# A perceiver kernel on one core: router scatters split into pairs, and the scale and bias of the contexts' layer norm given to GpSimd

## The chip, the core and the metric

The kernel runs on one core of a Trainium2 chip. The metric is the device time of one execution in microseconds (us). An execution moves through five engines that have their own instruction queues and wait for each other by semaphores: TensorE (PE in the profile; its weight loads are PEld), VectorE (DVE), ScalarE (ACT), GpSimd (POOL) and SyncE (SP), which here only issues DMA transfers. Each engine takes its instructions in the order in which the program lists them: an instruction that has to wait holds everything behind it on that engine.

## The reference

The inputs are latents x of 64 batches of 32 rows of 256 numbers, and for each batch a context of 257 rows of 256. In float32 the reference computes six residual steps in a row:

```python
x = x + cross_attention_1(context, norm(x))   # 16 heads of 64, with layer norms, q and k normed
x = x + self_attention_1(norm(x))             # 16 heads of 16
x = x + mixture_of_experts(norm(x))           # router: 8 of 64 experts a row, and a shared expert
x = x + cross_attention_2(norm(x), context)   # 16 heads of 64, softmax
x = x + self_attention_2(norm(x))             # latent heads, causal
x = x + ffn(norm(x))
```

Two pieces of it matter here. In the first cross-attention every context row is normed and then scaled and shifted by two vectors g and b of 256 numbers:

```python
def layernorm(x, g, b, eps=1e-05):
    m = jnp.mean(x, axis=-1, keepdims=True)
    v = jnp.mean((x - m) ** 2, axis=-1, keepdims=True)
    return (x - m) / jnp.sqrt(v + eps) * g + b
```

In the mixture of experts a router chooses 8 experts for each of the 2048 rows, and the row is copied to a slot of each chosen expert:

```python
w, idx = jax.lax.top_k(probs, TOP_K)
buf = jnp.zeros((E, CAPACITY + 1, H), x.dtype).at[e_flat, slot].set(x[tok])
```

## The kernel before

The 2048 latent rows are 16 tiles (t) of 128 rows, so four batches to a tile. The program has three stages. `before` does the first cross-attention batch by batch, and in its gaps the first self-attention and the router, tile by tile. `experts` runs the 64 experts and the shared one. `after` does the rest. The change lies in `before`.

The loop of `before` runs over the 64 batches (s; the profile's tiles name a batch's context `cx`). It is a software pipeline whose order is written out by hand. In step s it issues: the keys of batch s+2 (`keys`: 16 products of L180 into `psA`, copied by ACT at L1256 and DVE at L1258 into `kT`, squared by ACT at L1261 into `sq`); the transposes of batch s's softmaxed scores (`weigh`, L220, copied at L221); the norms of the keys of s+2 (`norms`: PE L1273, then DVE L1281, then ACT L1282); the values of batch s (`values`: PE L234 and L244); the spread of those norms (`spread`: PE L1294, then ACT L1295); the transposes of context s+3 (`turn`: PE L1228, ACT L1231, and two small copies by POOL at L1232 and L1233); the scores of s+2 (PE L1313, DVE L1323 and L1324, and the softmax with DVE L195, ACT L197, DVE L200 and L203, then DVE L210 and ACT L208); and last `prepare(s + 4)`, the layer norm of the context of s+4. So a context that is prepared in step s is transposed in step s+1.

`prepare` takes a context as two blocks of 128 rows by 256. DVE takes the statistics (L143, L145, L132), ACT makes 1/sqrt(variance) out of them (L133, L134), and then DVE makes four passes of 128x256: for each block L1215 subtracts the mean and multiplies by g, and L1216 multiplies by 1/sqrt and adds b.

The rest of the work hangs in between as Python generators. `slot()` goes once through the lists `tails` and `fronts` and runs each generator to its next `yield`. A front makes the queries of a coming tile (`queries`: DVE L154, POOL L1148 and L1149, DVE L1168 and L1169, POOL L1177, and the mask with POOL L1199 to L1201). A tail is what is left of a tile: the output product and its bias (POOL L185, DVE L186), self-attention (POOL L560 among it), and last `route`. Once the router's probabilities are there, `route` counts the slots (POOL L648), makes 8 row numbers (DVE L651 to L664, the last of them `fi`) and issues 8 scatters of 128 rows from POOL's queue (L667).

The order on PE is the program's own order. On the other engines a list scheduler of the language layer reorders the instructions at build time by its own estimates and by priorities (`with self.urgent()` raises one). It also chooses between DVE and ACT for copies that are written as `nc.any`. What the order on DVE, ACT and POOL becomes is thus not seen in the source.

Of the kernel before, what the change touches and what calls it, by code (L numbers as in the profile page):

```python
# [14 lines left out]
ALU = mybir.AluOpType  # L15
AX = mybir.AxisListType

P = 128
D = 256
# [14 lines left out]
TOPK = 8  # L34
# [67 lines left out]
class Kernel:  # L102
# [506 lines left out]
    def route(self, t, gw):  # L609
        nc = self.nc  # L610
        z, zT = yield from self.normed(t)
        nc.sync.dma_start(self.zs[t // GT][:, :, t % GT, :], zT)
        ps = self.bank("psA")
        self.product(
            ps[:, : E + 1],
            [zT[:, k, :] for k in range(2)],
            [gw[:, k, :] for k in range(2)],
        )

        sgt = self.sgate[:, t : t + 1]  # L620
        nc.scalar.activation(sgt, ps[:, E : E + 1], AF.Exp, scale=-1.0)
        nc.vector.tensor_scalar(sgt, sgt, 1.0, None, ALU.add)
        nc.vector.reciprocal(sgt, sgt)
        mx = self.small.tile([P, 1], F32, name="mx1")
        sm = self.small.tile([P, 1], F32, name="sm1")
        nc.vector.tensor_reduce(mx, ps[:, :E], AX.X, ALU.max, negate=True)
        pr = self.wk.tile([P, E], F32, name="pr")
        nc.scalar.activation(pr, ps[:, :E], AF.Exp, bias=mx, accum_out=sm)
        nc.vector.reciprocal(sm, sm)
        nc.vector.tensor_scalar(pr, pr, sm, None, ALU.mult)  # L630
        top = self.small.tile([P, TOPK], F32, name="top")
        nc.vector.max(top, pr)
        sel = self.wk.tile([P, E], F32, name="sel")
        nc.vector.match_replace(sel, top, pr, -1.0)
        nc.vector.tensor_scalar(sel, sel, 0.0, None, ALU.is_lt)
        tot = self.small.tile([P, 1], F32, name="tot")
        nc.vector.tensor_reduce(tot, top, AX.X, ALU.add)
        nc.vector.reciprocal(tot, tot)
        nc.vector.tensor_scalar(pr, pr, tot, None, ALU.mult)

        yield
        yield

        ps = self.bank("psA")
        self.product(ps[:, :E], [self.tri, self.ones], [sel, self.count])
        kept = self.wk.tile([P, E], F32, name="kept")
        nc.vector.scalar_tensor_tensor(kept, ps[:, :E], float(CAP), sel, ALU.is_lt, ALU.mult)
        nc.gpsimd.tensor_tensor(self.count, self.count, sel, ALU.add)  # L648
        val = self.wk.tile([P, E], F32, name="val")
        nc.vector.tensor_tensor(val, ps[:, :E], self.slot, ALU.add)  # L650
        nc.vector.tensor_tensor(val, val, kept, ALU.mult)  # L651
        v8 = self.small.tile([P, TOPK], F32, name="v8")
        nc.vector.max(v8, val)
        junk = self.wk.tile([P, E], F32, name="junk")
        for k in range(TOPK):
            nc.vector.scalar_tensor_tensor(
                junk, val, v8[:, k : k + 1], pr, ALU.is_equal, ALU.mult, accum_out=self.w8[:, t, k : k + 1]
            )
        nc.vector.tensor_copy(self.idx[:, t, :], v8)
        far = self.small.tile([P, TOPK], F32, name="far")  # L660
        nc.vector.tensor_scalar(far, v8, 0.0, FAR, ALU.is_equal, ALU.mult)
        nc.vector.tensor_tensor(far, far, v8, ALU.add)
        fi = self.small.tile([P, TOPK], I32, name="fi")
        nc.vector.tensor_copy(fi, far)  # L664

        for k in range(TOPK):
            d = nc.gpsimd.indirect_dma_start(  # L667
                out=self.buf[:, :],
                out_offset=bass.IndirectOffsetOnAxis(ap=fi[:, k : k + 1], axis=0),
                in_=z[:, 0, :],  # L670
                in_offset=None,
                bounds_check=E * CAP,
                oob_is_err=False,
            )
            self.tc.declare_no_dep(d.ins, group="scatter", reason="rows differ")
            self.tc.add_to_no_dep_group("scatter", d.ins)

    def experts(self, ctx, slot, tails):
        tc, nc, a = self.tc, self.nc, self.a
# [449 lines left out]
class CrossFirst:  # L1129
# [79 lines left out]
    def prepare(self, s):  # L1209

        k, nc, cx = self.k, self.k.nc, self.cx[s]
        mv, rs = k.stats(cx, 2)
        for j in range(2):
            x = cx[:, j, :]
            nc.vector.scalar_tensor_tensor(x, x, mv[:, j, 0:1], self.gx, ALU.subtract, ALU.mult)  # L1215
            nc.vector.scalar_tensor_tensor(x, x, rs[:, j : j + 1], self.bx, ALU.mult, ALU.add)  # L1216

    def turn(self, s):

# [308 lines left out]
```

## Time and profile before

| what | value |
|---|---|
| median of three runs | 2818.46 us (2815.7 to 2818.79) |
| the profiled execution, own time | 2816.43 us |
| its span, first to last instruction | 2814.2 us |
| mean granted TensorE clock | 0.984 |
| busy share of the span: PE, PEld, DVE, ACT, POOL | 94%, 65%, 62%, 44%, 19% |

The profile is one execution, so durations of single instructions come from it. The stage that the change touches lies between 0 and about 1465 us; the experts follow it. "Idle before, releaser" in a view says which instruction ended an engine's wait. PE is the engine to watch: a microsecond on another engine counts only where PE comes to wait for it. One tile of four batches takes 94 us in the middle of the stage, so one batch takes about 23.6 us.

### The profile page before, as it was taken

What the parts mean: (1) busy time and instruction counts of PE and PEld (TensorE: products, weight loads), DVE (VectorE), ACT (ScalarE), POOL (GpSimd) and SP (SyncE); (2) the same over time, 40 slices, a digit from 0 to 9 for tenths busy, and PEclk for the clock granted to TensorE, in tenths of its full rate; (3) what the DMA queues carried; (4) which work ended last, traced back from release to release, by engine and by line L of the source; (5) the groups of instructions that cost most, each with busy time, mean ns of one, the idle gap of its engine ahead of it and who ended that gap; (6) DMA issues with size and microseconds to landing.
All of it is one profiled execution on the core that took longest, in us unless ns stands there. A gap on an engine that the chain in (4) does not pass through costs nothing. (4 is left out here: it accounts for less than half of the span.)

```text
span 2814.2 us, 59449 instructions
## 1 busy us (share of the span) xinstructions
PE 2657.5 (94%) x23642; PEld 1824.2 (65%) x23642; DVE 1737.1 (62%) x4557; ACT 1235.0 (44%) x3474; POOL 541.5 (19%) x644
## 2 busy tenths in 40 slices
PE   6999999999999999999997889899999999999995
PEld 4566656665666566656664578677777777777763
DVE  6565656665666567656754533556666666666664
ACT  4555555555555555555553333333333333333331
POOL 3110122112211221122112200421222222121001
PEclk9999999999999999999998999999999999999997
DMA  7000001001110000000002388221212222221110
GB/s 262 27 16 14 18 31 33 31 18 31 32 30 18 27 26 22 18 19 19 17 5 86 130 270 269 83 72 48 61 48 58 52 55 59 51 57 47 33 33 7
DMA packets 136088, 157.05 MB, mean 56 GB/s; under 512 B 24024, under 2 KB 118979, under 8 KB 135812
## 3 DMA queue, kind: packets, MB, share of 16 engines
q1 hardware_dynamic: 114308, 119.65, 13.8%
q0 software_dynamic: 12288, 25.21, 3.5%
q10 hardware_dynamic: 9216, 8.39, 0.9%
q8 instruction: 187, 3.06, 0.5%
q14 instruction: 89, 0.73, 0.1%
HBM read 121.63 MB, written 37.75 MB: 57 GB/s over the span
## 5 line engine op out<-in xcount | busy, mean ns | idle before, releaser
L180 PE MATMUL psA<-xT,wk 128*128 128x289 f32 x2048 | 528.0, 413 | 16.6 <-issue 12.3
L180 PEld LDWEIGHTS psA<-xT,wk 128*128 128x128 f32 x2048 | 386.7, 192 | 151.6 <-issue 46.2
L828 POOL DMA_INDIRECT y<-oute,idx x128 | 131.0, 1024 | 646.2 <-DVE x L839 466.5
L234 PE MATMUL psY<-at,cx 128*128 128x512 f32 x512 | 237.6, 607 | 0.0
L180 PE MATMUL psY<-xT,qk 128*128 128x257 f32 x1024 | 233.7, 381 | 0.0
L180 PE MATMUL psA<-at,cx 128*128 128x512 f32 x512 | 233.5, 599 | 0.0
L180 PEld LDWEIGHTS psY<-xT,qk 128*128 128x128 f32 x1024 | 190.0, 190 | 25.2
L1414 ACT ACTIVATE sim<-psY,mx 128x257 f32<-128x257 f32 x256 | 120.6, 476 | 149.0 <-DVE mx L1413 148.0
L234 PEld LDWEIGHTS psY<-at,cx 128*128 128x128 f32 x512 | 92.6, 191 | 122.4 <-issue 99.0
L197 ACT ACTIVATE sim<-sim,mx 128x289 f32<-128x289 f32 x256 | 135.5, 532 | 63.9 <-DVE mx L195 63.7
L180 PEld LDWEIGHTS psA<-at,cx 128*128 128x128 f32 x512 | 93.4, 190 | 96.5 <-issue 83.2
L1261 ACT ACTIVATE sq<-kT 128x1156 f32<-128x1156 f32 x128 | 148.5, 1160 | 11.6 <-DVE kT L1258 10.5
L246 ACT COPY yT<-psY 128x512 f32<-128x512 f32 x128 | 68.7, 589 | 191.0 <-PE psY L244 191.0
L1323 DVE TENSOR_TENSOR sim<-psB,sim 128x289 f32<-128x289 f32 x256 | 100.8, 451 | 81.1 <-remote 27.9
L1256 ACT COPY kT<-psA 128x289 f32<-128x289 f32 x256 | 99.2, 388 | 116.8 <-PE psA L180 114.7
L667 POOL DMA_INDIRECT buf<-z,fi x128 | 126.3, 986 | 96.2 <-DVE fi L664 53.9
L1258 DVE COPY kT<-psA 128x289 f32<-128x289 f32 x256 | 114.5, 450 | 45.3 <-PE psA L180 45.0
L1413 DVE TENSOR_REDUCE mx<-psY 128x1 f32<-128x257 f32 x256 | 100.9, 417 | 52.9 <-PE psY L180 52.7
L180 PE MATMUL psY<-yT,wv 128*64 128x128 f32 x2048 | 126.3, 275 | 7.3 <-DVE yT L1444 7.3
L180 PEld LDWEIGHTS psY<-yT,wv 128*64 128x64 f32 x2048 | 114.9, 137 | 16.3 <-DVE yT L1444 11.2
L186 DVE TENSOR_TENSOR x<-x,psY 128x256 f32<-128x256 f32 (+1 forms) x80 | 29.2, 364 | 154.0 <-PE psY L180 152.4
L180 PE MATMUL psY<-wo,oT 128*128 128x128 f32 (+1 forms) x768 | 124.2, 315 | 0.0
(262 smaller groups left out, 5021.2 us busy)
## 6 DMA issues: line engine op xcount, KB each, us to landing
cx<-in_ctx SPq DMA_DIRECT2D x128, 256.0 KB
we<-in_m_ew SPq DMA_DIRECT2D x64, 384.0 KB
xT<-in_ctxT SPq DMA_DIRECT2D x64, 257.0 KB
buf<-zero SPq DMA_DIRECT2D x32, 256.0 KB
be<-buf SPq DMA_DIRECT2D x64, 128.0 KB
oute<-oe ACTq DMA_DIRECT2D x64, 128.0 KB
mu<-in_mask SPq DMA_DIRECT2D x16, 128.5 KB
x<-in_x SPq DMA_DIRECT2D x16, 128.0 KB
```

The lines of the kernel that those rows point to most:

```text
L180: self.nc.tensor.matmul(ps, lhsT=lhs[i], rhs=rhs[i], start=(i == 0), stop=(i == n - 1))
L197: nc.scalar.activation(sim[:, g, :], sim[:, g, :], AF.Exp, bias=mx[:, g : g + 1], accum_out=sm[:, g : g + 1])
L234: nc.tensor.matmul(ps[kc], lhsT=values[i][:, kc * P : (kc + 1) * P], rhs=at[i], start=(i == 0), stop=(i == n - 1 and tail is None),)
L246: nc.any.tensor_copy(yT[:, kc, :, b * S : (b + 1) * S], ps[kc].rearrange("p (h i) -> p h i", h=H))
L667: d = nc.gpsimd.indirect_dma_start(out=self.buf[:, :], out_offset=bass.IndirectOffsetOnAxis(ap=fi[:, k : k + 1], axis=0), in_=z[:, 0, :], ...
L828: nc.gpsimd.indirect_dma_start(out=y, out_offset=None, in_=self.oute[:, :], in_offset=bass.IndirectOffsetOnAxis(ap=self.idx[:, t, k : k + ...
L1256: nc.scalar.copy(kT[:, p, :], ps[:, :JK])
L1258: nc.vector.tensor_copy(kT[:, p, :], ps[:, :JK])
L1261: nc.scalar.activation(sq[p // 4], kT[:, p - 3 : p + 1, :], AF.Square)
L1323: nc.vector.tensor_tensor(sim[:, g, :], ps[i][:, :JK], sim[:, g, :], ALU.mult)
L1413: nc.vector.tensor_reduce(mx[:, g : g + 1], ps[:, :J], AX.X, ALU.max, negate=True)
L1414: nc.scalar.activation(sim[:, g, :], ps[:, :J], AF.Exp, bias=mx[:, g : g + 1], accum_out=sm[:, g : g + 1])
```

## The change

Two edits. The first puts a `yield` behind the second, fourth and sixth scatter of a tile, for all tiles but the last two. The second replaces the four DVE passes of `prepare`. DVE norms each block in one pass through the common helper (`layernorm`, whose pass is L154 in the profile before), and POOL then multiplies both blocks by g in one instruction of 128x512, and adds b in another.

```diff
@@ route
             self.tc.add_to_no_dep_group("scatter", d.ins)
+            if k % 2 and k < TOPK - 1 and t < self.nt - 2:
+                yield
@@ CrossFirst.prepare
         k, nc, cx = self.k, self.k.nc, self.cx[s]
-        mv, rs = k.stats(cx, 2)
-        for j in range(2):
-            x = cx[:, j, :]
-            nc.vector.scalar_tensor_tensor(x, x, mv[:, j, 0:1], self.gx, ALU.subtract, ALU.mult)
-            nc.vector.scalar_tensor_tensor(x, x, rs[:, j : j + 1], self.bx, ALU.mult, ALU.add)
+        k.layernorm(cx, cx)
+        nc.gpsimd.tensor_tensor(cx, cx, self.gx.unsqueeze(1).to_broadcast([P, 2, D]), ALU.mult)
+        nc.gpsimd.tensor_tensor(cx, cx, self.bx.unsqueeze(1).to_broadcast([P, 2, D]), ALU.add)
```

The two POOL instructions stand at L1215 and L1216 of the changed source, the lines that the four DVE passes had before; between the two edits all line numbers are two higher.

## The prediction

> **What bounds the kernel now.** I read the page first, then the stage that the change touches in one window, then PE's waits in it.
>
> ```profile
> PE 2657.5 (94%) x23642; PEld 1824.2 (65%) x23642; DVE 1737.1 (62%) x4557; ACT 1235.0 (44%) x3474; POOL 541.5 (19%) x644
> 100.00:1465.00 1365.00, 1330.86 (x11345) 849.67 (x11347) 885.92 (x2464) 734.62 (x2031) 271.29 (x354) 0.99 0.08 22
> PE psA L180 <- issue: 11.5, 33, 0.7
> PE psB L1313 <- ACT qTf L1193: 6.7, 15, 1.7
> PE psB L1273 <- ACT sq L1261: 5.7, 8, 1.0
> PE psT L163 <- issue: 3.8, 6, 1.0
> PE psB L1313 <- issue: 3.5, 11, 0.4
> PE psA L180 <- ACT xT L1231: 2.2, 4, 0.7
> PE psB L594 <- ACT yT L246: 0.2, 1, 0.2
> ```
>
> The window row gives the busy time of PE, PEld, DVE, ACT and POOL in 1365 us: PE 97.5%, DVE 65%, POOL 20%. The rows below it are all of PE's waits in that window (us in total, times, longest): 33.6 us. None names POOL, none names DVE. So the stage is PE's, and nothing that makes DVE lighter can win more than part of 33.6 us, while whatever makes PE's suppliers late costs at once. The next question is how late a supplier may be.
>
> ```profile
> 641.09 1.18 PE L1273 MATMUL psB<-sq,c 128*32 128x289 f32 x16
> 643.06 0.45 DVE L1281 TENSOR_SCALAR nk<-psB 128x289 f32<-128x289 f32 x1
> 643.55 0.45 ACT L1282 ACTIVATE nk<-nk 128x289 f32<-128x289 f32 x1 [1.76 <-DVE nk L1281]
> 646.89 0.77 PE L1294 MATMUL psR<-nk,c 32*128 32x289 f32 x8
> ```
>
> These four rows of the timeline (start, duration) are the chain of the key norms in the batch of a tile in which the router runs. ACT is done at 644.00, PE needs it at 646.89: 2.89 us in hand. In the batch before it (L1282 at 620.15, L1294 at 622.90) it is 2.30 us. All else that DVE hands over is asked for a batch (23.6 us) later.
>
> **First edit: the scatters.** In the built program's POOL order the eight scatters of every tile still stand in one row, before and after: the scheduler puts them together whatever the yields say. So it does nothing to PE, whose order is the same instruction for instruction. What remains: a tail lives three slots longer and holds `z` and `fi` longer; z's buffer is next wanted some four slots later, and the last two tiles, which the experts wait for, are exempt. Price 0. Were a `z` held too long, DVE's next L154 would wait; I give that 2 us at most, and no gain, since POOL sat idle 77 us before these scatters in the window.
>
> **Second edit: the passes.** The rows for what goes and for what is near to what comes (count, busy us, mean ns):
>
> ```profile
> L1216 DVE SCALAR_TENSOR_TENSOR cx<-cx,rs,a_bx 128x256 f32<-128x256 f32 x112 | 58.6, 546 | 1.6
> L1215 DVE SCALAR_TENSOR_TENSOR cx<-cx,mv,a_gx 128x256 f32<-128x256 f32 x112 | 52.3, 476 | 0.0
> L154 DVE TENSOR_SCALAR z<-x,mv,rs 128x256 f32<-128x256 f32 x27 | 11.0, 407 | 0.0
> L560 POOL TENSOR_TENSOR qk<-qk,sg 128x256 f32<-128x256 f32 x14 | 10.1, 724 | 81.6 <-DVE qk L559 81.6
> L1177 POOL TENSOR_TENSOR q<-q,ss x16: 1901/2497/3022, 29.9 to 1413.0; 128x1024 f32<-128x1024 f32 x16
> L185 POOL TENSOR_TENSOR x<-x,a_bo x28: 452/453/1507, 103.0 to 1373.4; 128x128 f32<-128x128 f32 x28
> ```
>
> DVE loses 64 x (2 x 0.476 + 2 x 0.546) = 130.8 us and gets 128 x 0.407 = 52.1 us: 78.7 us lighter, about 1.2 us a batch. That lies wholly beside PE, so by itself it is worth 0.
>
> POOL gets 128 products and sums of 128x512. The undisturbed rows are 128x128: 0.452, 128x256: 0.72, 128x1024: 1.90 us. From 128 to 256 an element costs 2.1 ns, which makes 512 elements 1.26 us; between 256 and 1024 a straight line gives 1.11. Here the Trainium skill speaks against the change: GPSIMD Engine Reference, section Performance versus the Vector engine, has such arithmetic at half of VectorE's speed, and 4497 ns for 2048 elements; from 0.72 at 256 that is 2.1 ns an element again, so 1.26. L1177's second operand is one number per head, repeated, so it is the less alike; I take 1.26 us, 161 us in all. POOL then works 432 of 1365 us, which is no bound.
>
> The cost is not POOL's time but a lock. In the timeline the pair of L1216 takes 0.88 us when POOL is idle, and beside POOL's L1148 and L1149 this:
>
> ```profile
> 637.66 0.88 DVE L1216 SCALAR_TENSOR_TENSOR cx<-cx,rs,a_bx 128x256 f32<-128x256 f32 x2
> 621.02 1.61 DVE L1216 SCALAR_TENSOR_TENSOR cx<-cx,rs,a_bx 128x256 f32<-128x256 f32 x2
> ```
>
> The other way round L185 took 1.507 instead of 0.453 us when it began inside DVE's L1324. So a DVE pass from SBUF to SBUF and a POOL operation exclude each other: who comes second waits for the end of the first. L1258 and L195 are not touched by it. The change makes 128 POOL operations against which DVE's L154, L210, L1324 and the router's small passes (L651, L661) can run, each up to about 1.1 us. If half of them meet one, DVE gives back some 70 us, all that it won.
>
> Where does that reach PE? In the router's batch the built POOL order has two context pairs (5 us) right ahead of the eight scatters, and DVE's queue has the router's passes and L1281 behind them. Against the rows of before, DVE is spared three passes of 0.48 (1.4 us) there, gets one L154 (0.4) and one L656 more (0.4), and waits for POOL about twice in full (2 x 1.1) and once in part (0.5): L1281 comes 2.1 us later, and of 2.89 us are left 0.8. In the batch before it the built order moves L1281 from ahead of L154 to behind three L154, the last of which waits for L1148: start 619.67 becomes about 621.1, L1282 ends at 622.05, and 0.85 of 2.30 are left; it is nearer 0.3 if ACT's 1/sqrt for the context comes 0.5 us later. Both are so near zero that some tiles must spill. I price it at 0.3 us for each of 13 tiles: 4 us; from 0 to 1.5 us a tile it is 0 to 20. With 1.11 us a POOL operation each full wait is 0.15 shorter and the spill is 0; that is the weight of the skill's figure: +3 by the row of L1177, +7 by the page.
>
> **Moved with it.** Queue orders change only up to 1465 us; behind that every engine's order is the same, so the later stages cost 0. The scheduler, having a lighter DVE, puts ACT's L208 ahead of the second `sq` in the third and the fifth batch. In the trace that `sq` began at once and PE still waited for it:
>
> ```profile
> 66.63 1.17 ACT L1261 ACTIVATE sq<-kT 128x1156 f32<-128x1156 f32 x1
> 67.85 1.17 PE L1273 MATMUL psB<-sq,c 128*32 128x289 f32 x12 [0.27 <-ACT sq L1261]
> ```
>
> L208 needs DVE's L203 (ends at 66.86) and takes 0.54, so `sq` begins at 67.45: 0.8 us straight onto PE, more if the lock holds L203 back. Two such places, and the first `sq` behind one L197 as well: 3 us; bounds 1 and 5. Some copies change engine (12 of L221 and 12 of L266 from DVE to ACT, 12 of L604 and 13 of L164 back): about +5 us of ACT's busy time in 1365, priced at 0 because PE asks for them later; the range has 3 us either way. Waits behind POOL's queue: scatters start some 1.1 us later (644.09 becomes about 645.2) and with them the xT copies behind them, which the key product 23 us later needs; L1177 waits for ACT until 657.9 anyway. At the start the first transposes of a context are at 24.7 us, and its two POOL operations can end by 20.5, behind the 6.7 us of query products. If that cover were gone, it would cost 2.5 us once. SP's loads keep their order but for a few early rows, and a context's buffer is freed by the same product: 0.
>
> **Sum.** 0 + 4 + 3 = +7 us on an execution of 2816.43 us (span 2814.2 and 2.2 around it). That execution lies 2.0 under the median of the runs, 2818.46; on the median it makes 2825.5 us.
>
> **Rivals.**
> *The lock is hidden* (0.20): L1281 stays inside its slack in both batches and only the early batches pay, while the spared passes return a little; -3 to +4 us, 2819. For it: 0.8 us are left by my count. Against it: my count has waits of 1.1 us in it, and one more uses all.
> *The lock decides in both batches of each tile* (0.17): one further full wait each, 1.1 us beyond the slack, 2 x 13 x 1 = 26 us and the 3: 2847. For it: the stacked pairs ahead of the scatters. Against it: DVE is 35% idle in the stage.
> *Faster* (0.13): of PE's waits, the 15 us named "issue" before L180 and L1313 are PSUM banks that DVE or ACT frees late. A DVE that is 1.2 us a batch lighter frees them sooner; with two thirds of that and no spill it is -10 + 3: 2811. It decides as soon as the lock gives back less than some 30 us of the 79. Against it: L1258 and L1323, which free those banks, are urgent already, and the longest of these waits is 0.7 us.
> *That the pairs of scatters come to nothing* is no rival but the forecast.
>
> **How the numbers follow.** The forecast itself (+3 to +14 us) has 0.50. What a measurement can tell here is about 0.2%, 5.6 us. A fifth of the forecast lies below that, so within 0.2% is 0.20 + 0.10 = 0.30, faster 0.13, slower 0.57. The range for eight in ten leaves out most of the faster case and the end of the double spill: 2813 to 2848.
>
> **What would show it.** Right: eight L667 in a row with about 0.3 us between them; L1215 and L1216 on POOL at 1.2 to 1.4 us; DVE's busy time between 100 and 1465 us about 810 to 880; L154 on contexts well over 0.41 in the mean; L1281 in the two batches 1.5 to 3 us later after L1273; PE with new waits at L1294 for ACT L1282 and more at L1273 for `sq`; everything after 1465 us merely shifted. Wrong: L1294 without waits and PE's waits in the stage down from 33.6 us (then the faster rival), or a PE that waits for POOL by name.

## The result, and the profile after

| | before | after |
|---|---|---|
| median of the runs | 2818.46 us (3 runs), with later runs 2815.7 to 2818.79 | 2833.12 us (5 runs, 2829.87 to 2838.95) |
| the profiled execution: own time, span | 2816.43, 2814.2 us | 2833.12, 2831.3 us |
| ratio after to before | | 1.0064, 95% interval 1.0053 to 1.0075 |

The change makes the kernel slower by 0.64%. The medians are 14.7 us apart, the profiled spans 17.1 us. The forecast was +7 us: the right direction, half of the size. The median lies in the stated range (2813 to 2848 us); how much of that was luck is said below.

The page of after (engines), its window row and PE's waits in the stage (us in total, times, longest):

```profile
PE 2654.6 (94%) x23642; PEld 1820.6 (64%) x23642; DVE 1721.5 (61%) x4429; ACT 1237.0 (44%) x3474; POOL 708.7 (25%) x772
100.00:1465.00 1365.00, 1315.86 (x11276) 836.50 (x11283) 863.11 (x2332) 731.10 (x2018) 415.95 (x468) 1.00 0.08 22
PE psB L1273 <- ACT sq L1261: 23.1, 15, 2.2
PE psA L180 <- issue: 15.0, 40, 0.8
PE psB L1313 <- ACT qTf L1195: 6.8, 15, 2.0
PE psA L180 <- ACT xT L1231: 1.7, 3, 0.7
PE psT L163 <- issue: 0.5, 1, 0.5
PE psB L594 <- ACT yT L246: 0.2, 1, 0.2
```

PE's waits went from 33.6 to 47.3 us (the waits are of the window 100 to 1480 us, as the same work ends later). In this window nothing names POOL, and L1294 is not in the list. The row that grew most is the second `sq`, from 5.7 us in 8 waits to 23.1 in 15; L180's "issue" grew from 11.5 to 15.0, and L163's and L1313's (3.8 and 3.5) all but went. To see where the time was lost, each matmul of after was set beside the same matmul of before (their order is the same); the lag grows in three places:

| stretch, by the time of before | after minus before, us |
|---|---|
| 0 to 185 us, the first batches | +6.4 |
| 185 to 1465 us, 13 tiles of steady work | +6.4 |
| 1465 to 2600 us | -0.5 |
| 2600 us to the end | +4.8 |

Three places, three causes. The steady one is seen in the batch behind the router's. The timeline of before, and then of after, in the same batch of the same tile (start, duration, operation, and in brackets the idle time before it and what ended it):

```profile
641.83 0.28 DVE L656 SCALAR_TENSOR_TENSOR junk<-val,v,pr 128x64 f32<-128x64 f32 x1
643.63 0.17 DVE L664 CAST fi<-far 128x8 int32<-128x8 f32 x1
644.09 1.08 POOL L667 DMA_INDIRECT buf<-z,fi  x1 [4.30 <-DVE fi L664]
649.94 1.20 PE L1313 MATMUL psB<-kT,qTf 64*32 64x289 f32 x30
655.79 1.56 DVE L1323 TENSOR_TENSOR sim<-psB,sim 128x289 f32<-128x289 f32 x4 [4.21 <-PE psA L180]
656.08 0.37 ACT L164 COPY zT<-psT 128x256 f32<-128x256 f32 x1 [3.99 <-PE psA L180]
```

```profile
649.07 0.93 DVE L656 SCALAR_TENSOR_TENSOR junk<-val,v,pr 128x64 f32<-128x64 f32 x1
650.00 1.29 POOL L1216 TENSOR_TENSOR cx<-cx,a_bx 128x512 f32<-128x512 f32 x1
650.08 1.29 DVE L656 SCALAR_TENSOR_TENSOR junk<-val,v,pr 128x64 f32<-128x64 f32 x1
651.63 0.17 DVE L664 CAST fi<-far 128x8 int32<-128x8 f32 x1
652.08 1.09 POOL L667 DMA_INDIRECT buf<-z,fi  x1 [0.79 <-DVE fi L664]
656.88 1.20 PE L1313 MATMUL psB<-kT,qTf 64*32 64x289 f32 x32
662.11 0.46 DVE L1323 TENSOR_TENSOR sim<-psB,sim 128x289 f32<-128x289 f32 x1 [3.58 <-PE psA L180]
662.83 0.46 DVE L1323 TENSOR_TENSOR sim<-psB,sim 128x289 f32<-128x289 f32 x1 [0.26 <-PE psA L180]
663.65 0.83 DVE L1323 TENSOR_TENSOR sim<-psB,sim 128x289 f32<-128x289 f32 x2 [0.36 <-PE psA L180]
671.27 0.68 PE L1273 MATMUL psB<-sq,c 128*32 128x289 f32 x4
672.02 0.54 ACT L208 ACTIVATE sim<-sim,sm 128x289 f32<-128x289 f32 x1 [0.35 <-DVE sim L203]
672.46 1.15 ACT L1261 ACTIVATE sq<-kT 128x1156 f32<-128x1156 f32 x1
673.66 1.17 PE L1273 MATMUL psB<-sq,c 128*32 128x289 f32 x12 [1.71 <-ACT sq L1261]
```

In both, PE's L1313 is over some 4 us before DVE's L1323 begins, and DVE and ACT sit idle together, both waiting for PE. What they read are its L163 and L1313, which were issued some 4 us earlier; the views name L180 because it is the last that PE had done by then. That was in the profile before, and the prediction did not ask why. The end of it does not go with PE: the last L1323 is let go 12.8 us behind the tile's first scatter in before and 12.2 in after (medians of 12 tiles). From there DVE and ACT need 8.4 us in both to the second `sq`, and PE waits for it. (On ACT an L208 stands ahead of this `sq` in before as well.)

And the first scatter comes 2.2 us behind the router batch's L1273 in before, 3.3 in after (counted, here and below, from the start of the last of its 16 products). It does not wait for a place in POOL's queue: in all 12 tiles of after POOL has been idle for 0.79 us when the scatter starts, and what ends that wait is `fi`. DVE makes `fi` late, 3.0 us behind L1273 instead of 1.9, because its small router passes meet the two POOL operations of a context. The rows above have two L656 at 0.93 and 1.29 us where before has 0.28.

Three theories were tested. S (signals): while a tile's scatters write, PE's signals reach DVE and ACT late, and the change moves the scatters 1.1 us later. L (lock): DVE passes are stretched by POOL wherever they meet, and that alone delays PE. O (order): ACT's L208 stands ahead of the second `sq`. S and L are less apart than they were taken to be, since it is the lock that makes `fi` late.

### The profile page after: what moved, and what is told of

Read it like the earlier page. It is cut to its first block, busy times and chain, and to the rows that moved or that the text cites. A ratio compares the mean times of both kernels' runs of the same rounds, so it can differ in the third digit from the quotient of the medians.

```text
span 2831.3 us, 59403 instructions
## 1 busy us (share of the span) xinstructions
PE 2654.6 (94%) x23642; PEld 1820.6 (64%) x23642; DVE 1721.5 (61%) x4429; ACT 1237.0 (44%) x3474; POOL 708.7 (25%) x772
## 3 DMA queue, kind: packets, MB, share of 16 engines
q1 hardware_dynamic: 114308, 119.65, 13.7%
q8 instruction: 187, 3.06, 0.4%
## 5 line engine op out<-in xcount | busy, mean ns | idle before, releaser
L180 PE MATMUL psA<-xT,wk 128*128 128x289 f32 x2048 | 524.9, 410 | 22.1 <-issue 15.0
L180 PEld LDWEIGHTS psA<-xT,wk 128*128 128x128 f32 x2048 | 383.3, 190 | 157.0 <-issue 50.5
L234 PE MATMUL psY<-at,cx 128*128 128x512 f32 x512 | 238.9, 610 | 0.0
L180 PE MATMUL psA<-at,cx 128*128 128x512 f32 x512 | 233.5, 599 | 0.0
L180 PE MATMUL psY<-xT,qk 128*128 128x257 f32 x1024 | 233.4, 380 | 0.0
L180 PEld LDWEIGHTS psY<-xT,qk 128*128 128x128 f32 x1024 | 189.7, 190 | 25.0
L1215 POOL TENSOR_TENSOR cx<-cx,a_gx 128x512 f32<-128x512 f32 x64 | 88.0, 1375 | 437.5 <-DVE cx L154 428.9
L234 PEld LDWEIGHTS psY<-at,cx 128*128 128x128 f32 x512 | 93.1, 191 | 123.2 <-issue 109.7
L197 ACT ACTIVATE sim<-sim,mx 128x289 f32<-128x289 f32 x256 | 135.7, 533 | 74.0 <-DVE mx L195 73.8
L180 PEld LDWEIGHTS psA<-at,cx 128*128 128x128 f32 x512 | 93.4, 190 | 96.5 <-issue 83.2
L1323 DVE TENSOR_TENSOR sim<-psB,sim 128x289 f32<-128x289 f32 x256 | 102.1, 452 | 86.7 <-PE psA L180 47.9
L667 POOL DMA_INDIRECT buf<-z,fi x128 | 126.6, 989 | 54.1 <-issue 33.6
L180 PE MATMUL psY<-yT,wv 128*64 128x128 f32 x2048 | 128.0, 277 | 7.3 <-DVE yT L1444 7.3
L180 PEld LDWEIGHTS psY<-yT,wv 128*64 128x64 f32 x2048 | 116.7, 138 | 16.3 <-DVE yT L1444 11.2
L180 PE MATMUL psY<-wo,oT 128*128 128x128 f32 (+1 forms) x768 | 124.2, 315 | 0.0
```

Of the source, the lines that this page charges most:

```text
L180: self.nc.tensor.matmul(ps, lhsT=lhs[i], rhs=rhs[i], start=(i == 0), stop=(i == n - 1))
L197: nc.scalar.activation(sim[:, g, :], sim[:, g, :], AF.Exp, bias=mx[:, g : g + 1], accum_out=sm[:, g : g + 1])
L234: nc.tensor.matmul(ps[kc], lhsT=values[i][:, kc * P : (kc + 1) * P], rhs=at[i], start=(i == 0), stop=(i == n - 1 and tail is None),)
L667: d = nc.gpsimd.indirect_dma_start(out=self.buf[:, :], out_offset=bass.IndirectOffsetOnAxis(ap=fi[:, k : k + 1], axis=0), in_=z[:, 0, :], ...
L1215: nc.gpsimd.tensor_tensor(cx, cx, self.gx.unsqueeze(1).to_broadcast([P, 2, D]), ALU.mult)
L1323: nc.vector.tensor_tensor(sim[:, g, :], ps[i][:, :JK], sim[:, g, :], ALU.mult)
```

## The experiments

"Before" was run again beside each set. The sets did not all run on one chip (e1 to e4 and e8 to e11 ran on chip 5 of the record, e5 to e7 on chip 12, e12 on chip 10): the median of before was 2812.04 us for e1 to e4, 2753.92 for e5 to e7, 2812.38 for e8 to e11, and 2815.63 for e12. That spread turned out to be part of the answer.

### e1 and e2: no scatters

```diff
-        for k in range(TOPK):
+        for k in range(TOPK if t >= self.nt - 2 else 0):
             d = nc.gpsimd.indirect_dma_start(
```

e1 is this in the kernel before, e2 in the changed one.

> The kernel before, with the eight scatters of the first 14 tiles left out (the rows of those tiles never reach the experts' buffer); every other instruction and the orders of PE, DVE, ACT and SP stay. Theory S, signals: while the scatters write, PE's signals to DVE and ACT arrive late (L1323 starts 4.1 us behind the last L1313 in every tile), so without them the gap at L1323 falls from 4.1 us to under 0.5 us, PE's waits named issue (11.5 + 3.8 + 3.5 us) and for the second sq (5.7 us) go: 2790 to 2803 us, 15 to 28 less than before. Theory L, lock of DVE and GpSimd: scatters play no part, 2816 to 2819 us. Theory O, order on ACT: the same as L.

> The changed kernel with the same scatters left out, all else as in the changed kernel. S: the steady loss of the change goes with the scatters, what stays is the start of the stage (about 4 us up to 100 us): 2 to 6 us over the kernel before without scatters. L: the lock's cost stays, 12 to 17 us over the kernel before without scatters. O: the same as L, for the order of ACT is kept.

Measured: e1 2752.01 us, 0.9782 of before (0.977 to 0.9795), 60 us less. e2 2767.72 us, 0.9842 (0.9829 to 0.9854). PE's waits from 185 to 1465 us, in e1 and then in e2:

```profile
PE psB L1313 <- ACT qTf L1193: 5.1, 14, 1.7
PE psA L180 <- ACT xT L1231: 0.5, 1, 0.5
PE psB L594 <- ACT yT L246: 0.2, 1, 0.2
```

```profile
PE psB L1313 <- ACT qTf L1195: 4.6, 14, 1.3
PE psB L1273 <- ACT sq L1261: 0.8, 1, 0.8
PE psA L180 <- ACT xT L1231: 0.2, 1, 0.2
```

And from the groups of e2:

```profile
L154 DVE TENSOR_SCALAR cx<-cx,mv,rs 128x256 f32<-128x256 f32 x114 | 55.7, 531 | 2.1 <-ACT rs L134 2.1
```

The scatters cost the kernel before 60 us, more than twice what S expected (15 to 28): its PE lost not only the waits that the views name (23 us of them went) but also time between matmuls. Without scatters, L1323 starts 1.56 us behind the first L1313 (5.85 before), and the steady stretch is 52.9 us shorter than the profiled before in e1 and 53.0 in e2: equal. L154 is as stretched by POOL in e2 (531 ns) as in after. So the lock is there, and without scatters it costs PE nothing in the steady part: L as it was put falls there. But the whole of e2 is 15.7 us over e1. S expected 2 to 6, and by this number alone L (12 to 17) would have been right. The two profiled runs are only 9.3 us apart, and of these 4.2 lie ahead of 185 us and 6.9 behind 2600 us; where the other 6 us of the medians lie is not shown. The tail was in no theory; see below.

### e3: the norm alone

```diff
         k.layernorm(cx, cx)
-        nc.gpsimd.tensor_tensor(cx, cx, self.gx.unsqueeze(1).to_broadcast([P, 2, D]), ALU.mult)
-        nc.gpsimd.tensor_tensor(cx, cx, self.bx.unsqueeze(1).to_broadcast([P, 2, D]), ALU.add)
```

> The changed kernel without the two GpSimd operations per context: the contexts are normed, but not scaled by g and shifted by b. Orders of PE, DVE, ACT and SP are those of the changed kernel. S: the first scatter comes about 5.8 us ahead of L1313 again, as before, so the steady loss goes; 2816 to 2823 us, the start's 4 us or less being left. L: below before, since DVE is also 79 us lighter: 2808 to 2818 us. O: the loss stays, 2828 to 2834 us.

Measured: 2801.98 us, 0.9961 of before (0.9949 to 0.9973), 10 us less. By the sum alone that is the edge of what L expected (0 to 10 less). But the trace has the first scatter 0.65 us behind L1273 (2.2 in before), the last L1323 12.7 us behind the scatter as ever, and PE without a gap at L1273. S was right about the place and wrong about the size: it expected the scatters 5.8 us ahead of L1313, and they are 7.4 ahead. A DVE with fewer passes and no POOL in its way has `fi` ready earlier than before. This run also prices the lock: DVE has the same passes in the same order as in after, and from the start of `kept` to the end of `fi` they take 2.2 us instead of 4.8 (medians of 12 tiles). The lighter DVE alone would have brought the scatters forward by 1.6 us; POOL's two operations push them back by 2.6. The early batches still wait 7.2 us for `sq`, against 3.3 in before: with no POOL operation on a context, that speaks for the order on ACT, O.

### e4: the scatters later, nothing else

```diff
+        late = self.wk.tile([P, TOPK, 64], I32, name="late", bufs=1)
+        nc.gpsimd.tensor_copy(late, fi.unsqueeze(2).to_broadcast([P, TOPK, 64]))
         for k in range(TOPK):
...
-                out_offset=bass.IndirectOffsetOnAxis(ap=fi[:, k : k + 1], axis=0),
+                out_offset=bass.IndirectOffsetOnAxis(ap=late[:, k, 0:1], axis=0),
```

> The kernel before with one more GpSimd operation per tile between fi and the scatters (a copy of fi spread to 128x512, from which the scatters take their row numbers): the scatters start 1.1 to 1.4 us later, DVE keeps its four passes per context. S: L1323's last release moves with the scatters, the second sq comes 0.5 to 1.3 us later against PE in 13 tiles: 6 to 14 us slower, 2824 to 2832 us. L and O: 16 short operations are all that is added, 2818 to 2820 us.

Measured: 2823.25 us, 1.004 (1.0026 to 1.0054), 11 us slower. The copy takes 0.61 us, so the scatters are only 0.7 us later. One small POOL operation per tile, in front of the scatters, does to PE's waits what the change does, with DVE's four passes untouched. The profiled runs place less of it than the medians: e4's is 4.6 us longer than before's, 1.6 of it in the steady stretch and 4.3 between 1465 and 2100 us. PE's waits in its stage (100 to 1440 us; lines are two higher):

```profile
PE psB L1275 <- ACT sq L1263: 21.2, 14, 2.6
PE psA L180 <- issue: 13.1, 39, 0.9
```

### e5 to e7: a chip on which nothing is held up

e5 is the changed kernel with part of the contexts given back to DVE, e6 the kernel before with pairs of scatters that are really apart, e7 the kernel before with the router's passes urgent. In e5 the four DVE passes stand ahead of the `return`; in e6 `tick` counts the batches and holds their `nk`.

```diff
 e5
+        if s < 6 or s % 4 == 2:
+            mv, rs = k.stats(cx, 2)
...
+            return
 e6
         for k in range(TOPK):
+            if paired and k % 2 == 0:
+                for _ in range(16):
+                    if self.tick[0] >= n0 + (k // 2 + 1 if k else 0):
+                        break
+                    yield
...
+                    nc.vector.scalar_tensor_tensor(
+                        far[:, k : k + 2], self.tick[1][:, 0:2], 0.0, far[:, k : k + 2], ALU.mult, ALU.add
+                    )
...
 e7
+        with self.urgent():
             kept = self.wk.tile([P, E], F32, name="kept")
...
```

> The changed kernel, but the first six contexts and every context s with s % 4 == 2 (the one whose pair of GpSimd operations stands right ahead of the scatters) keep the four DVE passes. S, signals late while the scatters write: the scatters start about 5.8 us ahead of L1313 again as in the kernel before, and the start of the stage is as before: within 4 us of before. L, lock of DVE and GpSimd wherever they meet: two thirds of the pairs are left, so 8 to 12 us slower than before.

> The kernel before with scatters that are really apart: for the first 13 tiles the row numbers of each later pair are made by DVE out of far plus zero times the key norms nk of a later batch, so one pair of L667 goes out per batch and POOL's order has 2+2+2+2 (the router's z has a buffer of its own). S: a pair writes for about 3 us instead of 11, so PE's signals are late by at most that, and most have that much in hand: of the 60 us that leaving the scatters out won, 25 to 55 come back, 2757 to 2787 us at 2812 for before. If the hold-up is by number of packets and has no slack to hide in: same total, within 5 us of before.

> The kernel before with DVE's passes from kept to fi (L646 to L664) raised in priority by the program's own urgent(): one small pass and the rest move ahead of L1281 and of a context's pass, so the scatters start 0.5 to 1 us earlier. S: 0.4 to 0.8 us per tile less, 5 to 11 us faster than before. L and O: no change, within 2 us.

Measured, against 2753.92 us for before: e5 2757.85 us, 1.0018 (1.0008 to 1.0027); e6 2763.57, 1.004 (1.0027 to 1.0054); e7 2753.32, 1.000 (0.9991 to 1.0008). e5 is where S put it (within 4 us); e6 and e7 are not, e7 being where L and O had it, and e7's timeline shows a reason for both. It has eight scatters in a row (L668), right through L1313:

```profile
635.47 0.97 POOL L668 DMA_INDIRECT buf<-z,fi  x1 [0.30 <-issue]
636.46 1.20 PE L1314 MATMUL psB<-kT,qTf 64*32 64x289 f32 x32
636.75 0.97 POOL L668 DMA_INDIRECT buf<-z,fi  x1 [0.30 <-issue]
638.02 1.54 DVE L1324 TENSOR_TENSOR sim<-psB,sim 128x289 f32<-128x289 f32 x4
638.03 0.97 POOL L668 DMA_INDIRECT buf<-z,fi  x1 [0.31 <-issue]
```

DVE's pass (here L1324) follows PE's first L1314 by 1.56 us, as without scatters. In this set the scatters hold nothing up, so the kernel before is 58 us faster without any change, and S has nothing to work on: its misses here are no evidence against it, and the hit of e5 is none for it. e6's own loss is another: from 1400 to 1580 us PE waits 11.4 us for DVE's norm of the router's rows (3.8 in e7), which was put down to late pairs of the last tiles that still held their buffer (e10, with fewer pairs, has 3.8 again). e5 says little on the steady part for the same reason; its start is 4 us late, at a later batch than in after.

### e8 to e11: the same questions where signals are held up

e8 is the changed kernel again, e9 the changed kernel with a mended start, e10 is e6 with pairs for the first 11 tiles only (`paired = t < self.nt - 5`), e11 is e7 again.

```diff
 e9
-            if g % 2:
+            if g % 2 and act:
                 nc.scalar.mul(sim[:, g, :], sim[:, g, :], sm[:, g : g + 1])
...
+        if s < 2:
+            mv, rs = k.stats(cx, 2)
...
+            return
```

`act` is `s > 7`, so the first eight batches have no L208.

> The changed kernel once more, since before ran in 2754 us where L1323 came 1.6 us behind L1313 in spite of the scatters, and in 2812 us where it came late. S: two separate costs, about 6.4 us at the start of the stage everywhere (order of sq on ACT 5.3, the first context's wait for GpSimd 1.2), and 6 to 11 us in the steady part only where the scatters hold PE's signals up. So 4 to 10 us over before if before runs near 2754 us here, 12 to 18 us if near 2812 us. L: 12 to 18 us in both.

> The changed kernel with its start mended: the first two contexts keep the four DVE passes, and in the first eight batches DVE makes all four scalings of the softmax, so no L208 stands ahead of a second sq on ACT. O with S: the start's 6.4 us go: 5 to 8 us less than the changed kernel in the same call, and so within 3 us of before where signals are not held up, 6 to 12 over it where they are. L: nothing of the steady loss goes, and the start is not where it is made: within 3 us of the changed kernel.

> The kernel before with scatters really in pairs as in the earlier run, but only for the first 11 tiles, so that no late pair holds the router's z of the last tiles (that cost 7.9 us ahead of the experts). Where signals are not held up: within 3 us of before. Where they are: if a pair's hold-up hides in the slack, 20 to 48 us faster than before; if it goes by packets, no change.

> The kernel before with the router's passes urgent, once more: the scatters start 0.36 us earlier against PE. S: nothing where signals are not held up (within 2 us), and 0.3 us per tile, 3 to 6 us faster, where they are.

Measured, against 2812.38 us for before:

| | median us | ratio (95%) |
|---|---|---|
| e8, changed kernel | 2836.55 | 1.0089 (1.0074 to 1.0105) |
| e9, start mended | 2830.87 | 1.0062 (1.0049 to 1.0076) |
| e10, real pairs | 2765.40 | 0.9834 (0.9821 to 0.9847) |
| e11, router urgent | 2800.13 | 0.9954 (0.9941 to 0.9968) |

e8 is 24 us over before, more than S and L expected (12 to 18), and more than the 14.7 of the first comparison; in its profile the start takes 9.9 us, the steady stretch 8.4. e9 takes 5.7 us off the changed kernel, as O expected (5 to 8), but stays 18 us over before, where 6 to 12 were expected. Its lag at 185 us is 0.8 us where e8's is 9.9; in the steady stretch its profile loses 10.8 us, with more granted clock lost (12.0 us after 6.8 in e8), so the two profiled runs end only 1.1 us apart. e10 is the version that beats both kernels, before by 47 us and e8 by 71: with pairs really apart L1323 follows L1313 by 1.56 us again. So a pair in a batch delays nothing that the views show, where eight in a row do. e11 is 12 us faster for scatters that start 0.36 us earlier; S expected 3 to 6, so the place is right and the size again more than a straight line gives.

Put in order by the place of the first scatter, the traces give this (medians of 12 tiles, us; the fourth column is of the next batch, where 0.25 means no gap; the last runs on PE from L1273 in the router's batch to L234 in the next):

| kernel | first scatter behind L1273 | last L1323 behind it | longest step between L1273 starts | PE, L1273 to L234 |
|---|---|---|---|---|
| e1, e2: none | - | - | 0.25 | 21.5 |
| e3 | 0.65 | 12.7 | 0.25 | 24.1 |
| e11 | 1.86 | 12.2 | 1.54 | 24.8 |
| before | 2.22 | 12.8 | 0.71 | 25.8 |
| e4 | 2.89 | 12.3 | 1.85 | 26.0 |
| after | 3.29 | 12.2 | 2.12 | 26.2 |
| e10: pairs | 2.22 | 8.5 | 0.25 | 21.5 |
| e7: eight, the other chip | 1.86 | 8.9 | 0.20 | 21.6 |

The third column is nearly the same (12.2 to 12.8 here, 12.1 in e8 and 11.9 in e9) for all kernels with eight in a row where signals are held up, wherever PE is: the scatters set it. Before's row is lifted a little by PE's granted clock: in four of its tiles it fell to half for 3.4 us, 6.8 us lost in all between 100 and 1465 us, against 1.7 in after; the other eight tiles have 25.7 in the last column. That hid part of what the change costs.

### e12: the change with real pairs

> The changed kernel with scatters that are really in pairs for the first 11 tiles, as in the second run of real pairs, and with g and b on GpSimd as in the change. S and O: the steady loss goes with the eight in a row, the start's 6 us stay: 4 to 10 us above what the kernel before makes with real pairs (0.983 of before where signals are held up, so 0.985 to 0.987; where they are not, 1.002 to 1.006 of before). L: the lock's cost stays, 12 to 20 us above: 0.988 to 0.991.

Edit: `prepare` of the change in e10. Measured: 2782.47 us, 0.9887 of before (0.9868 to 0.9906). By its ratio that is in L's range, about 15 us above e10. The traces put it elsewhere: the spans are 11.9 us apart, of which 8.6 lie ahead of 185 us, 0.9 in the steady stretch (to 1404 us), and 2.5 behind 1600 us. The steady loss is gone with the eight in a row, although DVE's passes up to `fi` are as stretched as in after (4.8 us); start and tail are not.

### The tail

All queue orders are the same behind 1465 us, and still the last 200 us are longer by 3.5 to 6.6 us in after, e2, e8, e9 and e12, and by at most 1.1 us in the eight other kernels. PE's waits of after near its end (2773 to 2803 us) have two that before lacks, and the timeline has their places:

```profile
PE psY L324 <- issue: 2.3, 1, 2.3
PE psA L180 <- issue: 1.2, 1, 1.2
```

```profile
2780.56 3.17 PE L180 MATMUL psA<-wl,zT 128*128 128x512 f32 x7 [1.23 <-issue]
2795.06 0.34 PE L324 MATMUL psY<-eT,vz 32*32 32x32 f32 x11 [2.27 <-issue]
```

The page's DMA part has a line for what carries instructions:

```profile
q8 instruction: 187, 3.06, 0.4%
```

Its 187 packets have 16 KB each; 3.06 MB over PE's 47,899 recorded instructions works out at 64 bytes each, so I take it for PE's own stream. In after one such packet runs from 2778.20 to 2779.37 and PE goes on at 2780.56; another from 2792.44 to 2793.66, and PE goes on at 2795.06, 117 matmuls into a run of 128. In before the packets of this stretch lie elsewhere (2779.69, 2788.70) and PE doesn't stop. PE's lag behind before grows by 3.9 of the 4.8 us at these two stops. The rest falls just behind the second, where the granted clock stays at half for 13.7 us (6.8 in before).

What moved the packets is inferred. In before, 646 of PE's waits are instructions of their own; in the five kernels with the long tail it is 611 or 612, in the others 628, 646 or 648. Fewer waits ahead shift every later boundary of 256 instructions by some 34. That fits all 14 traces; it was not tested, for instance by padding PE's stream.

## Why the prediction was right or wrong

The median fell into the range partly by luck. Of the +7 us only the 3 at the start came where it was put, and by a mechanism that the runs bear out in part. The 4 us at L1281 did not come, and the loss that stands in their place had been priced at 0, as had the tail.

- *Scatters in pairs: 0.* Right. POOL has eight L667 in a row in after, and PE names none. What the edit was written to do is worth 47 us (e10), on chips that hold signals up; a `yield` doesn't do it, a data dependence does.
- *POOL operation 1.26 us.* Nearly: the first takes 1.26 us alone (at 24.95 us) and 1.39 and 1.29 in the mean of the stage.

```profile
L1215 POOL TENSOR_TENSOR cx<-cx,a_gx 128x512 f32<-128x512 f32 x57 | 79.0, 1386 | 419.9 <-DVE cx L154 412.5 <-PE psT L163 7.4
L1216 POOL TENSOR_TENSOR cx<-cx,a_bx 128x512 f32<-128x512 f32 x57 | 73.3, 1286 | 4.2
L656 DVE SCALAR_TENSOR_TENSOR junk<-val,v,pr 128x64 f32<-128x64 f32 x96 | 47.0, 489 | 1.7
```

- *The lock gives about 70 of 79 us back.* Near in size: DVE's busy time over the whole run falls by 15.6 us (1737.1 to 1721.5), so some 63 of 78.7 come back (roughly, since some copies changed engine as well); between 100 and 1465 us it is 863 us after 886. L154 on contexts takes 531 ns (442 in e3, without the POOL operations), L656 489 instead of 280. The lock was held to reach PE through L1281; it does not (no wait at L1294), and without scatters it does not reach PE in the steady part at all (e2). It reaches PE through `fi` and the scatters. So the estimate from the page's figure (the Trainium skill, GPSIMD Engine Reference, Performance versus the Vector engine; 1.26 us, against 1.11 by L1177's row) chose the better duration and moved a term that was empty.
- *L1281's chain spills: +4.* Wrong step. The sizes were right and the spill did not come:

```profile
648.02 1.18 PE L1273 MATMUL psB<-sq,c 128*32 128x289 f32 x16
652.30 0.45 DVE L1281 TENSOR_SCALAR nk<-psB 128x289 f32<-128x289 f32 x1
652.78 0.45 ACT L1282 ACTIVATE nk<-nk 128x289 f32<-128x289 f32 x1 [4.06 <-DVE nk L1281]
653.83 0.77 PE L1294 MATMUL psR<-nk,c 32*128 32x289 f32 x8
```

  L1281 begins 4.28 us behind L1273, 2.3 later than before (forecast 2.1), and 0.6 us are left. In the batch before it, it is 0.8 later, not 1.4. Pricing "some must spill" from two margins above zero was the error: each tile repeats within hundredths, so a margin above zero is a margin in every tile.
- *ACT order, +3 (bounds 1 and 5).* Right place, undersized: PE's waits for `sq` grow by 5.3 us at four early L1273, not two. With it the cover at the start was gone, which the prediction named with its price (2.5 us) and put at 0:

```profile
PE psB L1273 <- ACT sq L1261: 8.6, 5, 2.6
PE psA L180 <- POOL cx L1215: 2.7, 1, 2.7
```

  (after, 18 to 185 us; 3.3 us and none in before.) A PE that waits for POOL by name was one of the prediction's signs of being wrong; it came, but only at the start. The lag at 185 us is 6.4 us in after and 9.9 in e8; e9 shows that the two mends together take it away. They were not tried apart: in e9 the POOL wait is gone, but PE still waits 5.9 us for `sq` (9.0 in e8), 2.6 of it in the third batch, where no L208 stands ahead of the second `sq` any more. So L208 alone is not shown to be the cause; the first `sq` still begins behind one L197 there.
- *Scatters 1.1 us later: 0.* The step that failed most. The size of the move was right (1.07 us), its price was not. It was taken for a wait in POOL's queue, and what was asked was only who stands behind the scatters there; the first reading, that all else DVE hands over is asked for a batch later, had left out `fi`, which POOL waits for at once. Behind the scatters in time stood every engine that listens to PE. Measured +6.4 us in after, and +8.4 in e8, whose granted clock lost as much as before's (6.8 us).
- *Later stages: 0.* Failed by the tail, +4.8, for a reason that no queue order shows.
- The rivals: "the lock decides in both batches" was right in a loss of over 10 us, by a path that wasn't there (no wait at L1294). "Faster" had a grain of truth: e3, with a lighter DVE and no POOL pair, is 10 us faster, though through earlier scatters.

## What to carry to other kernels

When two engines go idle together for 4 us and wait for a third that is done, find out what else runs in that time before pricing anything: here that one line was worth 60 us, and moving the scatters by 1 us against it cost 6 to 8 us, while the work that was moved cost PE nothing in the steady part. Two engines that exclude each other need not meet on the critical path to cost time: look at what the stretched passes hand over, and to whom. A margin that repeats from tile to tile is either spilled always or never. To spread work that a scheduler packs, tie each piece to data that comes late; and run a comparison on more than one chip before trusting a size.

## What the runs showed of the hardware

- While eight scatters of 128 rows of 1 KB write (first packet 1.66, last 10.9 us behind the first scatter), DVE and ACT start on results of PE that look finished about 4 us late. The trace's record of PE's semaphore falls silent too: within 8 us behind L1313 its longest pause is 4.3 us in before and 1.0 in e1, e7 and e10 (medians of 12 tiles). In the set of e5 to e7 nothing is late, with as many packets at the same times, and before takes 2754 instead of 2812 us. The same kernel (e7, e11) takes 2753.32 and 2800.13 us. Only one chip in one set (chip 12) was without the hold-up, so whether it is the chip or, for instance, where the buffers lie in memory is open. So are two other things: whether PE's signal is late or the end of its matmul, since those ends are modelled in the profile, and whether it is the writing or POOL's own work on the scatters, which takes the same 10 us.
- PE stops 1.2 and 2.3 us near the end of after, and goes on 1.2 and 1.4 us after a 16 KB instruction packet is in. That it had run out of instructions there is inferred, not tested.
- POOL's arithmetic excludes DVE's L656 as well: 0.28 us (before, and e3 in the mean) becomes 0.93 and 1.29 beside a context's pair. That is what delays `fi`.
